# A decoder layer on one core: three fold pieces moved behind the gate's ranks, and quantizing's second step on ScalarE

## The chip, the cores and the metric

The kernel runs on one core of one Trainium2 chip, as one launch. The metric is the device time of an execution in microseconds; lower is better. It is given as the median of several runs.

## What is computed

Two layers of a decoder on four sequences of 512 rows with 256 features, in float32. Each of six blocks adds to the running `x` a function of its normalized rows:

```python
x = x + _L0_attn_ref(_layernorm(x, axis=-1), ...)     # causal mixing of 16 heads, a gated running sum
x = x + _L0_xattn_ref(_layernorm(x, axis=-1), ctx_768, ...)   # 16 heads, softmax over 512 keys
x = x + _L0_ffn_ref(_layernorm(x, axis=-1), ...)      # 8 experts and 4 "zero" experts, top two of a gate
x = x + _L1_attn_ref(_layernorm(x, axis=-1), ...)     # a gated recurrence over time
x = x + _L1_xattn_ref(_layernorm(x, axis=-1), ctx_768, ...)   # ternary weights, 8-bit activations
x = x + _L1_ffn_ref(_layernorm(x, axis=-1), ...)      # 8 linear experts, top two of a gate
```

Two pieces of it matter here. The experts of the last block have no function between their two matrices, so `(h @ w_in.T) @ w_out.T` can be computed with one 256 x 256 matrix per expert, the "folded" weight `w_in.T @ w_out.T`. And each linear map of the fifth block rounds its input to steps of the largest absolute value of the whole tensor:

```python
i_scale = jnp.maximum(jnp.max(jnp.abs(x)), 1e-08) / 127.0
qx = jnp.clip(jnp.round(x / i_scale), -128.0, 127.0)
out = jnp.einsum('...i,oi->...o', qx, qW) * (w_scale * i_scale)
```

The maximum is needed before the first value can be rounded, which makes each such map a stage of its own.

## The kernel before, in words

The program is written as Python functions that emit instructions. A scheduler then decides, for each engine, in which order its instructions stand in its queue; only instructions marked "in program order" (`pinned` matmuls, `move` transfers) keep the order of the source among themselves. Each engine runs its queue strictly in order. Tiles come from pools with a fixed number of buffers, and an instruction that needs a buffer waits until the last reader of its former content is done. So a small edit can move instructions elsewhere as well.

The stages, with their times in the profiled execution:

- **The frame** (`l0_mixers`, to about 560 us). The first two blocks are interleaved in 16 units `u` (sequence `u // 4`, a quarter of the heads each). A unit has eight slots `n`; in each slot scores are computed (PE, L588), reduced for their maximum (DVE `tops`, L927) and passed through an exponential (ACT `e`, L930); further work is hung into slots by `after(n, f, ...)` (around L1202). From unit 11 on this includes the **fold**: `fold_piece(i)` is one of four pieces of the folded weight of expert `i // 4`, four matmuls that the trace lists as eight rows (L588 `fold<-w_outT,w_in`). `fetch_fold(e)` loads the two weights of expert `e` (2 MB, four transfers in SP's queue, L595); they have two buffers, so expert `e` is fetched when expert `e - 2` has its last piece done. After an expert's fourth piece ACT copies the sum out (`folded`, L1091) and SP stores it (`far_folded`). Units 11 to 15 take four pieces each, 0 to 19, in slots 0, 1, 2 and 7.
- **The tail of the frame** (about 560 to 609 us, from L1352). The last sequence's results are added to `x`; then `Places` sorts its rows to the experts of the third block: `norm` (DVE), `transpose`, `score` (the gate's matmuls), `pick` (top two; `top_two`, L1399 to L1428, in which ACT computes `tt_share` at L1426 from DVE's `tt_gap`), `rank` (PE counts with `ranks`, L588; DVE then works out each row's place, L1550 to L1568), and `put` (GpSimd scatters rows into a table, one indirect transfer for 128 rows and one of its two experts). Between them stand pieces 20 to 22, 23, and, after the puts and `fetch_fold(7)`, pieces 24 to 31. A fence (L1597) waits for all the puts; the first expert's rows are read from the table behind it (L1632).
- **The experts** (`l0_experts`, 609 to 794 us). For each of eight experts: read its 640 rows, transpose them (PE `eturn` L1637, DVE copy `eht` L1638), first matrix (PE `ef<-eht,sw`), ACT `eact`, second matrix (PE `ef<-sw,eact`), DVE copy `ey` (L1668), store. Interleaved with it, through generators, stand the ternary weights (`Ternary`: a sum on DVE, a total on PE, comparisons on DVE) and the image side of the fifth block (`images`): quantize the context (`q_ctx`), matmuls `vis`, their maxima (`vis_tops`, L1897), quantize (`q_vis`), matmuls `img`, maxima and means, quantize (`q_img`), matmuls for the keys.
- **Gather and recurrence** (`l1_attn`, to about 948 us): rows are gathered from the table, then the fourth block.
- **The text side** (`l1_fuse`, to 1069 us): quantize the text (`q_txt`), matmuls `fused`, two attentions over the image keys (`bsc`, `bet`, `bav`), then quantize the result (`q_cat`).
- **The hidden stage** (`l1_hidden`, to about 1119 us): 32 matmul groups `hid`, for each a Relu on ACT (L2169) and a maximum on DVE (`hid_tops`, L1897); after the last of them quantize (`q_hid`, 16 slices of 128 x 1024, four a sequence), matmuls `bf`, and their sum into `x` (L2183).
- **The last block** (`l1_ffn`, to the end): the folded weights are read back (L2192), then norm, gate and the `y` matmuls.

`Steps.quantize(dst, src, tmp, on_act)` rounds in two steps through a temporary: multiply and add a large constant (which rounds), and subtract it again. The temporary `q_tmp` has two buffers in the stages where `on_act` is used. With `on_act` the first step runs on ACT, otherwise on DVE; the second runs on DVE in both cases. `on_act` is set for every other slice: two of the four slices of the text, two of `q_cat`, eight of the sixteen of `q_hid`. `q_ctx`, `q_vis`, `q_img` and the small `q_mean` don't use it.

Of the kernel before, what the change touches and what calls it, by code (L numbers as in the profile page):

```python
# [9 lines left out]
F32 = mybir.dt.float32  # L10
# [3 lines left out]
AF = mybir.ActivationFunctionType  # L14
# [4 lines left out]
P = 128  # L19
# [15 lines left out]
MAGIC = 12582912.0  # L35
# [6 lines left out]
class Kernel:  # L42


    def __init__(self, ctx, tc, a, out):
        self.ctx, self.tc, self.nc, self.a, self.out = ctx, tc, tc.nc, a, out
        nc = self.nc
        self.const = ctx.enter_context(tc.tile_pool(name="const", bufs=1))
        self.keep = ctx.enter_context(tc.tile_pool(name="keep", bufs=1))
        self.h_pool = ctx.enter_context(tc.tile_pool(name="h", bufs=2))  # L50
        self.small = ctx.enter_context(tc.tile_pool(name="small", bufs=4))
        self.open_psum()
        ctx.callback(self.close_psum)


        self.tops = self.keep.tile([P, 4 * NB, QT, 4], F32, name="tops")
        self.fine = self.keep.tile([P, 2 + 4 * (NB - 2)], F32, name="fine")

        self.most = self.keep.tile([P, 1], F32, name="most")

        self.rows = self.keep.tile([P, 2, NT], I32, name="rows")
        self.shares = self.keep.tile([P, 2, NT], F32, name="shares")
        self.fence = self.keep.tile([1, 1], F32, name="fence")
        self.puts = []
        self.table = ctx.enter_context(tc.tile_pool(name="table", bufs=1, space=bass.MemoryType.DRAM)).tile(
            [STAY + 2 * N, D], F32, name="table"
        )

        self.x = self.keep.tile([P, NT, D], F32, name="x_sb")
        self.load_x(0)  # L70

        self.ident = self.const.tile([P, P], F32, name="ident")
        make_identity(nc, self.ident)
        self.ones = self.const.tile([P, P], F32, name="ones_pp")
        nc.gpsimd.memset(self.ones, 1.0)
        self.magic = self.const.tile([P, 1], F32, name="magic")
        nc.gpsimd.memset(self.magic, MAGIC)


        self.by_head = self.head_of(self.const, "by_head", [P, 4, 16], [[P, 4], [-32, 16]], 1)  # L80
        self.iota12 = self.const.tile([P, 12], F32, name="iota12")
        nc.gpsimd.iota(
            self.iota12, pattern=[[1, 12]], base=0, channel_multiplier=0, allow_small_or_imprecise_dtypes=True
        )
        self.iota12_up = self.const.tile([P, 12], F32, name="iota12_up")
        nc.vector.tensor_scalar_add(self.iota12_up, self.iota12, 64.0)
# [454 lines left out]
def l0_mixers(k):  # L541
# [18 lines left out]
    nc, tc, a = k.nc, k.tc, k.a  # L560
    k.close_psum()
    far_folded(k)
    with ExitStack() as es:
# [11 lines left out]
        def bank(name):  # L575
            return ps_misc.tile([P, 512], F32, tag="bank", name=name)
# [7 lines left out]
        def pinned(out, pairs, start=True, stop=True):  # L584

            for i, (lhs_t, rhs) in enumerate(pairs):
                tc.keep_in_program_order(
                    nc.tensor.matmul(  # L588
                        out, lhs_t, rhs, start=start and i == 0, stop=stop and i == len(pairs) - 1
                    )  # L590
                )

        def move(dst, src):

            dma = nc.sync.dma_start(dst, src)  # L595
            tc.keep_in_program_order(dma)
            return dma
# [13 lines left out]
        ctxs, w, bias, padded = {}, {}, {}, {}  # L611
# [453 lines left out]
        def fetch_fold(e):  # L1065

            folds[e] = []
            for name in ("w_in", "w_outT"):
                t = k.fold_w.tile([P, 8, D], F32, tag=name, name=f"{name}_{e}", bufs=2)
                src = a[name][e].rearrange("(c p) d -> p c d", p=P)  # L1070
                for j in (0, 4):
                    move(t[:, j : j + 4], src[:, j : j + 4])
                folds[e].append(t)

        def fold_piece(i):

            e, c, j4 = i // 4, i // 2 % 2, i % 2 * 4
            if i % 4 == 0:
                folds[e].append(bank(f"fold_{e}").rearrange("p (c d) -> p c d", d=D))
                if e + 1 < 7:  # L1080
                    fetch_fold(e + 1)
            w_in, w_out, ps = folds[e]
            pinned(
                ps[:, c, :],
                [(w_in[:, j, c * P : (c + 1) * P], w_out[:, j, :]) for j in range(j4, j4 + 4)],
                j4 == 0,
                j4 == 4,
            )
            if i % 4 == 3:
                folded = k.fold_w.tile([P, DC * D], F32, tag="folded", name=f"folded_{e}", bufs=2)  # L1090
                nc.scalar.copy(folded.rearrange("p (c d) -> p c d", d=D), ps)  # L1091
                move(k.far_folded[e], folded)
# [122 lines left out]
        units = 4 * NB  # L1215
        for u in range(units + 1):
# [6 lines left out]
            def after(n, f, *args):  # L1223
                then[n].append((f, *args))
# [10 lines left out]
            if u == FOLDING:  # L1235

                mixers.close()
                k.fold_pool = ExitStack()
                k.fold_w = k.fold_pool.enter_context(tc.tile_pool(name="fold_w", bufs=2, side="right"))
                k.places = Places(  # L1240
                    k, k.fold_pool.enter_context(tc.tile_pool(name="places", bufs=1, side="right")),
                    move, bank, turn, pinned, new_ht,
                )
                after(7, fetch_fold, 0)
            elif u > FOLDING:
                if u < units:
                    for j, n in enumerate((0, 1, 2, 7)):
                        after(n, fold_piece, 4 * (u - FOLDING - 1) + j)
                g = k.places
                if u == 11:  # L1250
                    after(1, g.norm, 0)
                    for c in range(DC):
                        after(4 + c, g.transpose, 0, c)
                    after(5, g.norm, 1)
                    after(6, g.score, 0, (0, 1))
                elif u == 12:
                    for c in range(DC):
                        after(1 + c, g.transpose, 1, c)
                    after(3, g.score, 1, (0, 1))
                    after(4, g.pick, (0, 1))  # L1260
                    after(7, g.rank, (0, 1))
                elif u == 13:
                    for i in range(QT):
                        after(2 + i, project, 2, i)
                        after(3 + i, g.put, 0, i, weighing)
                    after(7, g.norm, 2)
                elif u == 14:
                    for c in range(DC):
                        after(1 + c, g.transpose, 2, c)
                    for i in range(QT):  # L1270
                        after(3 + i, g.put, 1, i, weighing)
                    after(3, g.score, 2, (2,))
                    after(3, g.pick, (2,))
                    after(6, g.rank, (2,))
                elif u == 15:
                    for i in range(QT):
                        after(3 + i, g.put, 2, i, weighing)
# [78 lines left out]
            xt = k.x[:, (NB - 1) * QT + i, :]  # L1356
            nc.vector.tensor_add(xt, xt, outs["xo"][:, i, :])
        places, last = k.places, NB - 1
        for i in range(20, 23):
            fold_piece(i)  # L1360
        places.norm(last)
        for c in range(DC):
            places.transpose(last, c)
        places.score(last, (last,))
        places.pick((last,))
        fold_piece(23)
        places.rank((last,))
        for i in range(QT):
            places.put(last, i)
        fetch_fold(7)  # L1370
        for i in range(24, 32):
            fold_piece(i)
# [6 lines left out]
FOLDING = 10  # L1379
# [473 lines left out]
class Steps:  # L1853
# [25 lines left out]
    def quantize(self, dst, src, tmp, on_act=False):  # L1879

        nc, p = self.k.nc, src.shape[0]
        t = tmp.tile(list(src.shape), F32, tag="q_tmp", name="q_tmp")
        if on_act:
            nc.scalar.activation(t, src, AF.Identity, scale=self.inverse[:p], bias=self.k.magic[:p])
        else:
            nc.vector.tensor_scalar(t, src, self.inverse[:p], MAGIC, ALU.mult, ALU.add)
        nc.vector.tensor_scalar_sub(dst, t, MAGIC)

    def scale_with(self, weight, pool, name):
        s = pool.tile([P, 1], F32, name=name)  # L1890
# [350 lines left out]


FAST = [l0_mixers, ahead, l0_experts, l1_attn, l1_xattn, l1_ffn]
GENERAL = [l0_attn, l0_xattn_clamped, ahead, l1_images, l0_ffn, l1_attn, l1_xattn, l1_ffn]

# [110 lines left out]
```

## Time and profile before

| what | value |
| --- | --- |
| runs: median (lowest to highest) | 1257.15 us (1253.43 to 1259.84) |
| the profiled execution: its time / its span | 1259.12 us / 1257.4 us |
| mean granted clock of TensorE | 0.887 of full speed |
| busy: PE / DVE / ACT / POOL | 79% / 65% / 33% / 15% |
| a fold piece (eight rows) | 1.99 us in the frame's end |
| quantize, first step, 128 x 1024: DVE / ACT | 748 ns / 1240 ns |
| quantize, second step on DVE | 688 ns |

The names of the engines: PE is TensorE's matmul (PEld its weight load), DVE is VectorE, ACT is ScalarE, POOL is GpSimd, SP is SyncE, whose queue issues most transfers. A row of the view by stretch gives, for a window in us from the span's start, its length and then the busy time of each engine with its count of instructions, the granted clock of TensorE, the busy share of the DMA engines and what they moved. A row of the timeline gives start, duration, engine, line, operation, output and inputs, the number of instructions in it, and in brackets how long the engine had been idle before and what ended that. A row of a tile's view gives the shortest, median and longest duration in ns and the starts of the first and last.

### The profile page before, as it was taken

The numbers are of one execution on the slowest core, as the hardware profiler recorded it, in microseconds if no ns is written. First come the engines' busy times: TensorE is split into PE (matmuls) and PEld (weight loads), VectorE is DVE, ScalarE is ACT, GpSimd is POOL, SyncE is SP. The second block draws the span as 40 slices with busy tenths as digits, with TensorE's granted clock in tenths as the row PEclk, the third lists the DMA queues.
The fourth block names the chain that finished last, engine by engine and source line by source line (L and its number), as shares of the span: only waits on it lengthen the run. The fifth ranks groups of instructions, "written<-read, shape, count | busy, mean of one in ns | idle before, by whom it ended". The sixth has DMA issues, their size and how long they took to land. (4 is left out here: it accounts for less than half of the span.)

```text
span 1257.4 us, 12049 instructions
## 1 busy us (share of the span) xinstructions
PE 996.7 (79%) x3865; PEld 560.1 (45%) x3871; DVE 815.4 (65%) x1980; ACT 417.0 (33%) x716; POOL 188.0 (15%) x224
## 2 busy tenths in 40 slices
PE   5889578688965999788689999336686777779997
PEld 1454333243332556547566677213453433254443
DVE  5776697777679767634365951437756665986564
ACT  4513345545443464430101421023323433820000
POOL 5431112113113002221000000450001220000000
PEclk9989787888976999888899999668887998879999
DMA  5385515333443635544557261220001110020000
GB/s 155 94 266 208 149 38 174 116 112 120 143 145 111 205 118 162 179 137 141 171 172 208 85 225 64 79 76 1 0 1 38 47 37 17 0 68 1 33 17 20
DMA packets 90779, 129.97 MB, mean 103 GB/s; under 512 B 20268, under 2 KB 61740, under 8 KB 90700
## 3 DMA queue, kind: packets, MB, share of 16 engines
q1 hardware_dynamic: 84544, 111.29, 28.3%
q0 software_dynamic: 6144, 17.83, 4.1%
q8 instruction: 33, 0.54, 0.2%
q14 instruction: 38, 0.31, 0.1%
q10 hardware_dynamic: 20, 0.00, 0.0%
HBM read 86.56 MB, written 42.53 MB: 103 GB/s over the span
## 5 line engine op out<-in xcount | busy, mean ns | idle before, releaser
L930 ACT ACTIVATE e<-score,tops 128x512 f32<-128x512 f32 x256 | 161.4, 685 | 171.8 <-DVE tops L927 99.3
L927 DVE TENSOR_REDUCE tops<-score 128x2 f32<-128x1024 f32 x128 | 155.8, 1219 | 44.4 <-PE score L588 39.6
L212 PE MATMUL y<-folded_sb,fht 128*128 128x512 f32 x256 | 113.4, 603 | 0.0
L588 PE MATMUL score<-query,key 64*128 64x512 f32 x256 | 67.8, 532 | 24.7 <-ACT e L930 21.3
L2212 DVE SCALAR_TENSOR_TENSOR x_sb<-y,tt_w,x_sb 128x256 f32<-128x256 f32 x128 | 61.9, 483 | 38.3 <-PE y L212 35.0
L965 PE MATMUL av<-e,weighed 128*32 128x512 f32 x512 | 77.8, 648 | 5.7 <-POOL weighed L953 5.7
L212 PE MATMUL ef<-sw,eact 128*128 128x256 f32 x320 | 79.4, 387 | 2.4 <-DVE ey L1668 2.4
L212 PE MATMUL ef<-eht,sw 128*128 128x320 f32 x256 | 76.7, 440 | 0.6 <-ACT eact L1657 0.6
L212 PEld LDWEIGHTS y<-folded_sb,fht 128*128 128x128 f32 x256 | 49.2, 194 | 60.3 <-issue 60.2
L588 PEld LDWEIGHTS score<-query,key 64*128 64x128 f32 x256 | 25.2, 197 | 100.9 <-ACT e L930 51.9
L212 PEld LDWEIGHTS ef<-sw,eact 128*128 128x128 f32 x320 | 58.7, 193 | 12.9 <-DVE ey L1668 5.1
L588 PE MATMUL fold<-w_outT,w_in 128*128 128x256 f32 x256 | 63.3, 397 | 0.5 <-PE fold L588 0.5
L203 PE MATMUL turn<-ident,h 128*128 128x128 f32 x64 | 13.7, 364 | 62.5 <-DVE h L190 42.1
L588 PE MATMUL o<-o_wT_sb,qk 128*128 128x256 f32 x128 | 47.1, 531 | 20.3 <-DVE qk L826 20.3
L212 PEld LDWEIGHTS ef<-eht,sw 128*128 128x128 f32 x256 | 47.8, 192 | 17.4 <-ACT eact L1657 1.2
L1657 ACT ACTIVATE eact<-ef 128x640 f32<-128x640 f32 x32 | 22.3, 702 | 100.0 <-PE ef L212 100.0
L588 PEld LDWEIGHTS fold<-w_outT,w_in 128*128 128x128 f32 x256 | 48.3, 196 | 9.5 <-issue 2.6
L588 PEld LDWEIGHTS o<-o_wT_sb,qk 128*128 128x128 f32 x128 | 32.8, 268 | 33.9 <-DVE qk L826 23.6
L212 PE MATMUL f<-aht,W_fT_sb 128*128 128x512 f32 x96 | 47.5, 644 | 0.1
L1638 DVE COPY eht<-eturn 128x256 f32<-128x256 f32 x40 | 16.8, 421 | 42.4 <-PE eturn L1637 42.2
L1740 POOL DMA_INDIRECT got<-table,rows x32 | 30.4, 949 | 85.9 <-DVE neg_b L1732 76.5
L179 DVE BATCH_NORM_STATS2 ln_st<-x_sb 128x6 f32<-128x256 f32 x96 | 38.1, 412 | 5.8 <-DMA x_sb<-in_x 3.8
(394 smaller groups left out, 1812.0 us busy)
## 6 DMA issues: line engine op xcount, KB each, us to landing
table<-zeros POOLq DMA_DIRECT2D x8, 1152.0 KB
factors<-far SPq DMA_DIRECT2D x64, 128.0 KB
key<-far_k SPq DMA_DIRECT2D x16, 512.0 KB
query<-far_q SPq DMA_DIRECT2D x16, 512.0 KB
w_in<-in_w_in SPq DMA_DIRECT2D x16, 512.0 KB
w_outT<-in_w_outT SPq DMA_DIRECT2D x16, 512.0 KB
rows<-table SPq DMA_DIRECT2D x8, 640.0 KB
table<-ey SPq DMA_DIRECT2D x8, 640.0 KB
```

Of the source, the lines that this page charges most:

```text
L179: nc.vector.bn_stats(st[:, i, :], s)
L203: nc.tensor.transpose(ps[:, i * P : (i + 1) * P], h[:, i, c * P : (c + 1) * P], self.ident)
L212: self.nc.tensor.matmul(out, lhs_t, rhs, start=(i == 0), stop=(i == len(pairs) - 1))
L588: nc.tensor.matmul(out, lhs_t, rhs, start=start and i == 0, stop=stop and i == len(pairs) - 1)
L927: nc.vector.tensor_reduce(top, ps, AX.X, ALU.max, negate=True)
L930: nc.scalar.activation(e[:, i, :], ps[:, i, :], AF.Exp, bias=top[:, i : i + 1])
L965: nc.tensor.matmul(avs[u][32 * h : 32 * h + 32, :], weighed[u % 2][:, j, h, :], es_of[u, h // 2, j][:, h % 2, :], start=(j == 0), stop=(j ...
L1638: nc.vector.tensor_copy(ht[:, :, i * P : (i + 1) * P], ps)
L1657: nc.scalar.activation(act[:, f, :].rearrange("p (j t) -> p j t", j=2), ps[:, :, :half], AF.Silu)
L1740: nc.gpsimd.indirect_dma_start(out=got[t, which], out_offset=None, in_=k.table, in_offset=bass.IndirectOffsetOnAxis(ap=k.rows[:, which, t ...
L2212: nc.vector.scalar_tensor_tensor(xt, ps[:, e, :], w[:, i, e4 + e : e4 + e + 1], xt, ALU.mult, ALU.add)
```

## The change

Three edits. A constant tile `less` holds the negative of the rounding constant. In the frame, unit 14 takes pieces 12 to 14 and unit 15 pieces 15 and 16, so 17 pieces instead of 20 lie in the units; in the tail pieces 17 to 19 stand where 20 to 22 stood, 20 where 23 stood, and 21 to 23 behind the ranks and puts, ahead of the fetch for expert 7. And where `on_act` is set, quantizing's second step is an Identity activation on ACT with `less` as its bias, instead of DVE's subtraction. From line 77 on every line of the changed kernel stands two to seven lines lower.

```diff
         self.magic = self.const.tile([P, 1], F32, name="magic")
         nc.gpsimd.memset(self.magic, MAGIC)
+        self.less = self.const.tile([P, 1], F32, name="less")
+        nc.gpsimd.memset(self.less, -MAGIC)
...
             elif u > FOLDING:
                 if u < units:
-                    for j, n in enumerate((0, 1, 2, 7)):
-                        after(n, fold_piece, 4 * (u - FOLDING - 1) + j)
+
+                    first = 4 * (u - FOLDING - 1) - (u == units - 1)
+                    for j, n in enumerate((0, 1, 2, 7)[: min(4, units + 1 - u)]):
+                        after(n, fold_piece, first + j)
...
         places, last = k.places, NB - 1
-        for i in range(20, 23):
+        for i in range(17, 20):
             fold_piece(i)
         places.norm(last)
         for c in range(DC):
             places.transpose(last, c)
         places.score(last, (last,))
         places.pick((last,))
-        fold_piece(23)
+        fold_piece(20)
         places.rank((last,))
         for i in range(QT):
             places.put(last, i)
+        for i in range(21, 24):
+            fold_piece(i)
         fetch_fold(7)
         for i in range(24, 32):
             fold_piece(i)
...
         if on_act:
             nc.scalar.activation(t, src, AF.Identity, scale=self.inverse[:p], bias=self.k.magic[:p])
+            nc.scalar.activation(dst, t, AF.Identity, bias=self.k.less[:p])
         else:
             nc.vector.tensor_scalar(t, src, self.inverse[:p], MAGIC, ALU.mult, ALU.add)
-        nc.vector.tensor_scalar_sub(dst, t, MAGIC)
+            nc.vector.tensor_scalar_sub(dst, t, MAGIC)
```

## The prediction

> **What bounds the kernel now.** I read the page's busy shares first (PE 79%, DVE 65%, ACT 33%), then busy time by stretch, because the share is an average over stages with different limits.
>
> ```profile
> core 0: us, PE busy (x) PEld busy (x) DVE busy (x) ACT busy (x) POOL busy (x), PEclk, DMA share, GB/s
> 528.00:547.00 19.00, 17.52 (x101) 10.27 (x99) 12.27 (x26) 9.50 (x17) 6.89 (x8) 1.00 0.50 163
> 547.00:560.00 13.00, 9.88 (x54) 4.92 (x55) 3.06 (x13) 3.37 (x7) 2.16 (x3) 0.74 0.65 208
> 586.00:609.00 23.00, 14.80 (x69) 12.54 (x70) 3.96 (x28) 1.17 (x2) 8.38 (x10) 0.92 0.81 266
> 690.00:735.00 45.00, 41.05 (x204) 28.54 (x207) 40.75 (x77) 16.52 (x23) 1.05 (x3) 1.00 0.34 115
> ...
> 1069.00:1091.00 22.00, 16.87 (x57) 5.32 (x56) 21.48 (x33) 21.18 (x32) 0.00 (x0) 0.97 0.00 0
> 1091.00:1120.00 29.00, 19.39 (x128) 13.60 (x128) 26.74 (x73) 9.93 (x8) 0.35 (x1) 0.78 0.01 1
> ```
>
> PE has idle time in the frame's end and in the tail (rows two and three). In 690–735 PE and DVE are both nearly full, so order decides. In 1069–1091 DVE and ACT are full together; in 1091–1120 DVE is, with ACT two thirds idle. Then the tail, PE first, then ACT, then DVE:
>
> ```profile
> 581.07 3.76 PE L588 MATMUL fold<-w_outT,w_in 128*128 128x256 f32 x8
> 586.38 0.39 PE L588 MATMUL ranks<-both,before 128*128 128x48 f32 x2 [1.55 <-DVE both L1533]
> ...
> 594.46 7.14 PE L588 MATMUL fold<-w_outT,w_in 128*128 128x256 f32 x32 [0.50 <-PE fold L588]
> 608.94 0.66 PE L1637 MATMUL eturn<-ident,rows 128*128 128x128 f32 x2 [7.33 <-DMA rows<-table]
> ```
> ```profile
> 584.91 0.58 ACT L1091 COPY folded<-fold 128x512 f32<-128x512 f32 x1 [6.91 <-issue]
> 585.39 0.21 ACT L1426 ACTIVATE tt_share<-tt_gap 128x4 f32<-128x4 f32 x1
> ```
> ```profile
> 583.53 0.15 DVE L1415 TENSOR_TENSOR tt_gap<-top,top 128x4 f32<-128x4 f32 x1
> 585.63 0.24 DVE L1428 TENSOR_SCALAR shares<-tt_share 128x4 f32<-128x4 f32 x2 [1.54 <-ACT tt_share L1426]
> ```
>
> tt_gap is done at 583.68, but tt_share is queued behind the copy of the fold, which waits for piece 23; DVE loses 1.54 us and the ranks with it. From the ranks hang the rows, the puts, the fence, and the read of the first expert's rows, for which PE stands idle 7.33 us.
>
> **The frame.** A piece is 8 matmul rows: 1.99 us, 2.53 at the slow clock. Three leave (525.71, 535.29, 544.83): 6.5 us of PE. PE doesn't set the end there: around these pieces it waits for POOL's `weighed` (1.09), DVE's `low` (0.87) and `diag` (2.30), so removal is worth no 6.5 us. In the new order DVE's `low` stands behind a row reduce, which can delay an `av` group by about 1.6; on the other side the 2.30 wait may shrink. Bounds −1.6 to +2. A rule speaks against the move: 548–552 is mostly idle and 552–556 ran at clock 0.50, where 32 `av` took 5.50 us (eight took 1.06 at full clock, so 32 should take 4.2). The Trainium skill, "TensorE: Matmul & The Clock Gate", Part 1, says that an idle window of some 3.4 us puts the array at half clock and that a busy one of that length restores it: filler taken out makes one more such window likely. By the row nothing is added, since that loss is already there; by the rule one more half-clock window costs an estimated 1.7. I take +0.5, nearer the row.
>
> **The tail.** Pieces 17–19 replace 20–22 in 569.4–574.8, beside DVE's normalization; piece 20 replaces 23. With tt_share ahead of the copy in ACT's queue, the ranks come 1.5 earlier (584.9). Pieces 21–23 (3 × 1.79 = 5.4) then run to 590.7, 24–27 to 597.8. SP: the fetch of expert 7's weights needs piece 23 and moves from 585.96 to some 591; 2 MB at the 350 GB/s of this stretch is 6 us, about 1 to land, so 28–31 start near 598.3 and end at 605.5. Rows land at 608.9 − 1.5 = 607.4: the 5.4 us are covered by PE's 7.33 of idle (without it they would cost all 5.4). SP's later loads (w1, w2 of expert 0, the copies of folded weights) stay ahead of the rows' read; the puts on POOL keep their eight 1.27 us slots but share the DMA engines with the fetch (±1). One thing takes the gain back: on PE the new order puts W_d2vT's total ahead of the first eturn. That weight is issued 0.41 us behind the rows, then DVE reduces it (0.67) and a matmul follows: eturn at about 607.4 + 0.4 + 0.7 + 0.5 = 609.0 against 608.94. Net 0, from −1.5 (no wait) to +2 (late rows).
>
> **The experts, whose source is untouched.** The compiled queues of the two kernels differ here: the image chain (q_ctx, vis, q_vis, img, q_img, keys) is interleaved about one expert earlier.
>
> ```profile
> L212 PE MATMUL vis<-q_ctx,W_d2vT_q x16: 376/377/381, 693.1 to 702.6; 96*128 96x512 bf16 x16
> ```
> ```profile
> L212 PE MATMUL img<-q_vis,W_imgT_q x15: 376/379/389, 707.6 to 717.2; 128*128 128x512 bf16 x15
> L1887 DVE TENSOR_SCALAR q_vis<-q_tmp x4: 683/695/695, 706.9 to 711.6; 128x1024 bf16<-128x1024 f32 x4
> ```
>
> Before, the first vis (693.13) to the first key (725.3) takes 32.2 us; PE has 31.2 us of work queued between, DVE about as much: balanced, 1 us lost. I add up the same durations along the new queues. PE has 23.7 us between first vis and first key, as less expert work lies between. DVE, from the first q_ctx to the first q_img: three pairs q_tmp/q_ctx 4.3, eight vis tops 5.4, two ey and two eht copies 1.9, step and its POOL reduce 1.2, first q_vis pair 1.4; then three pairs 4.3, eight img tops 5.4, four img_mean 5.0, copies 1.9, step 1.5, q_img 1.4: 33.7 in all. It leads by about 3.7, as q_ctx is ready while PE still has 5.8 us of other matmuls ahead of vis (less a 0.7 copy and the 1.4 pair). PE is starved 33.7 − 23.7 − 3.7 = 6.3 instead of 1.0: +5.3, and with 0.2 for a shorter cover elsewhere I take +5.5. The starved PE can't run expert 4 ahead: its eturn copies on DVE stand behind six img tops and three img_mean. The PE-only work behind the keys grows (77.6 us for 61.8), with DVE idle, so nothing is won back. Bounds: −3, if PE's waits ahead of vis (9.6 us before, 3.32 of them one eturn on DVE) shrink and nothing starves; +13, if the lead isn't there and those waits grow by 4.
>
> **Quantizing.** Twelve second steps leave DVE (0.69 each, 8.3 us) for ACT. ACT's f32-to-bf16 form isn't in the trace; nearest is the first step on ACT:
>
> ```profile
> L1887 DVE TENSOR_SCALAR q_hid<-q_tmp x16: 677/688/696, 1092.8 to 1113.3; 128x1024 bf16<-128x1024 f32 x16
> ...
> L1884 ACT ACTIVATE q_tmp<-hid,magic,hid_inverse x8: 1239/1240/1242, 1092.1 to 1110.0; 128x1024 f32<-128x1024 f32 x8
> ```
>
> Text: ACT's chain is 4 × 1.24 = 5.0 from 950.3, ready at 955.3, PE needs the last at 955.8: 0. Cat: ACT runs 4 × 1.24 from 1064.3, to 1069.3; the first Relu of `hid`, queued behind, began at 1068.68, and the stage after it is full on ACT and DVE: +0.6. Hid: before, 16 slices took from 1092.05 to 1114.0; now DVE has 1.44 per pair of slices and ACT 2.48, ACT sets the pace: 8 × 2.48 = 19.8, to 1112, with a little slack 1112.5. The last x_sb (1117.35) follows the last slice by 3.3, and the fetch of the folded weights (1118.69) hangs on it: −1.2. The Trainium skill, "ScalarE: Activation LUTs", on what ACTIVATE costs, has 280 ns + 0.833 per element with a pointer bias, and back-to-back overlap of 93 ns: an estimated 1.13 for the new step instead of the row's 1.24. By the page cat is 0 and hid −2.5, quantizing −2.5 in all; by the row −0.6. I take the row: the second step reads what the first has just written, so the page's overlap can't be counted on here; bounds −2.5 to +1. The y stage, PE-full, is untouched.
>
> **Sum.** 0.5 + 0 + 5.5 + 0.6 − 1.2 = +5.4 on the profiled execution's 1259.12 (span 1257.4 and 1.7 around it), so 1264.5. That execution lies 1.97 above the median of the runs, 1257.15: predicted 1262.5.
>
> **Rivals.** (a) *Clearly slower.* The same starvation in full: DVE gives no lead, because its ctx reduces stand between the eht copies there (as PE's 3.32 wait before vis does now). PE then loses 10 rather than 6.3 and 1–4 more ahead of vis: experts +11, sum +11, 1268. It decides from a lead under 2.5 us. For: the interleave of tops and eht in the new order; against: DVE was busy only 29 of 50 us just before. (b) *Faster.* PE's waits in the expert stage shrink because the early chain fills them, and the tail keeps its 1.5: experts −3, tail −1.5, frame −1, quantizing −2: −7.5, 1249.7. It decides from experts at 0 or below. For: 9.6 us of waits ahead of vis, ACT's copy that does leave the path; against: the sum of 33.7 on DVE. (c) *No effect*: experts 0 to +2, the other terms cancel; 1257. For: only little of the order in other stages moves.
>
> **Chances.** Forecast (its own range 1259 to 1266) 0.36, (a) 0.27, (b) 0.20, (c) 0.17. A measurement of this kernel tells about 0.5% (6.3 us) from no change: slower means over 1263.4, faster under 1250.9. The forecast straddles the upper bound, half of it on either side. Slower: (a) and that half, 0.45. Faster: nearly all of (b), 0.18. Same: the rest, 0.37. The range takes in most of (b) and of (a): 1250 to 1273.
>
> **What would show it.** Frame: first `att` work of the tail within 2 us of before. Tail: ranks before 585.5, PE's wait for rows about 2 us instead of 7.33, eturn within 2 us of 609. Experts: first vis near 689, first key near 719, PE's gaps between them waiting for q_vis, img and q_img. Hid: ACT back to back at about 1.24, last x_sb 1 us earlier relative to the stage's start. Wrong if the experts' stretch (609 to 794) doesn't get longer, if ACT's second step is far from 1.24, or if the rows land late.

## The result and the profile after

The changed kernel took 1269.42 us (median of 6 runs, 1266.45 to 1271.05) against 1256.54 us for the kernel before: a ratio of 1.0106, 95% interval 1.0078 to 1.0134. So it is slower by 1.1%, 13 us. The profiled execution took 1269.73 us with a span of 1268.0, 10.6 over the span of before. It lies outside the forecast's own range (1259 to 1266), at rival (a), 1268, and inside the stated range of 1250 to 1273.

Where the 10.6 us went, by the starts of the same instructions in both traces (the stretch from the first Relu to the first quantize of `hid`, not listed, took 23.3 in both):

| stretch | before | after | difference | predicted |
| --- | --- | --- | --- | --- |
| start to unit 13's `low` | 498.5 | 495.8 | -2.7 | 0 |
| unit 13's `low` to the first `xo` (frame's end) | 61.2 | 66.0 | +4.8 | +0.5 |
| first `xo` to the ranks | 26.7 | 23.6 | -3.1 | -1.5 |
| ranks to the first `eturn` | 22.5 | 25.5 | +3.0 | +1.5 |
| first `eturn` to the first gather (experts) | 190.0 | 203.7 | +13.7 | +5.5 |
| first gather to the first `fused` | 152.9 | 151.8 | -1.1 | 0 |
| first `fused` to the first Relu of `hid` | 116.9 | 117.3 | +0.4 | +0.6 |
| first quantize of `hid` to the first `y` | 34.2 | 30.8 | -3.4 | -1.2 |
| first to last `y` | 122.1 | 121.2 | -0.9 | 0 |

The first row is not the change's: the first units hold the same instructions, and the first `low` starts anywhere from 159.5 to 162.6 us in the twelve other traces, with the old fold and the new.

**The experts.** The rows by stretch of before and then of after, from the first eturn to the first gather:

```profile
608.90:798.90 190.00, 171.24 (x779) 127.04 (x782) 99.21 (x182) 40.93 (x57) 1.05 (x3) 0.97 0.45 144
```
```profile
610.80:814.50 203.70, 177.81 (x782) 129.97 (x782) 99.80 (x181) 41.25 (x57) 1.08 (x4) 0.94 0.41 131
```

PE runs nearly the same number of instructions, but it is busy 6.6 us longer with them, at a clock of 0.94 instead of 0.97, and it idles 25.9 us instead of 18.8, 7.1 more. These two are the 13.7. The timelines of the changed kernel show where, PE first, then DVE:

```profile
657.42 0.69 PE L1643 MATMUL eturn<-ident,rows 128*128 128x128 f32 x2 [4.29 <-DVE eht L1644]
...
680.78 0.44 PE L1643 MATMUL eturn<-ident,rows 128*128 128x128 f32 x2 [3.12 <-DVE eht L1644]
...
718.17 0.93 PE L214 MATMUL ef<-eht,sw 128*128 128x320 f32 x2 [3.75 <-DVE eht L1644]
719.09 1.22 PE L214 MATMUL ef<-sw,eact 128*128 128x256 f32 x2
...
722.36 4.82 PE L214 MATMUL ef<-sw,eact 128*128 128x256 f32 x14
```
```profile
652.55 4.48 DVE L1854 SCALAR_TENSOR_TENSOR W_f1T_q<-W_f1T_sb,W_f1T_half,W_f1T_low 128x4096 bf16<-128x4096 f32 x1
656.95 0.42 DVE L1644 COPY eht<-eturn 128x256 f32<-128x256 f32 x1
...
679.12 1.28 DVE L1904 TENSOR_REDUCE ctx_tops<-ctx_all 96x1 f32<-96x512 f32 x2 [3.37 <-DMA ctx_all<-in_ctxT]
680.31 0.41 DVE L1644 COPY eht<-eturn 128x256 f32<-128x256 f32 x1
...
714.25 3.46 DVE L1986 TENSOR_REDUCE img_mean<-img_t 128x2 f32<-128x1024 f32 x3
717.63 0.15 DVE L1869 TENSOR_REDUCE img_one<-img_tops 128x1 f32<-128x8 f32 x1
717.70 0.41 DVE L1644 COPY eht<-eturn 128x256 f32<-128x256 f32 x1
```

In each of the three places PE waits for a small eht copy, 0.41 us, which stands on DVE behind something else: a comparison of 4.48 us, the context's maxima, which had themselves waited 3.37 us for their transfer, and the image's sums. The second has its like before (3.32 us ahead of vis, also behind the context's maxima); the first and the third are new. After the third wait two `ef<-sw,eact` rows take 1.22 us, where two take 0.59 to 0.60 in the same trace at full clock, and fourteen take 4.82, where fourteen took 3.27 at 634.58. The rows by stretch behind the three waits show half the clock:

```profile
653.87:660.70 6.83, 3.28 (x10) 2.45 (x11) 4.94 (x5) 0.00 (x0) 0.00 (x0) 0.50 0.35 108
681.18:684.59 3.41, 3.41 (x10) 2.35 (x9) 2.25 (x6) 0.00 (x0) 0.00 (x0) 0.50 1.05 359
718.72:725.55 6.83, 6.46 (x21) 4.20 (x21) 6.62 (x13) 0.78 (x1) 0.00 (x0) 0.50 0.14 56
```

Together they are 17.1 us at half clock. Before, the clock was at half for 6.7 us from the first eturn (6.8 in the changed kernel), for 3.4 from 653.12, behind a wait of 2.93, and for the last 2.4, and nowhere else in the stage: the wait of 3.32 was followed by full clock. So the clock's loss came on top of the waits here, but not every wait of this length brings it.

**The frame's end**, PE in the changed kernel:

```profile
531.96 0.37 PE L939 MATMUL low<-ident,low 128*4 128x128 f32 x1 [2.57 <-DVE works L1569]
532.13 3.71 PE L590 MATMUL fold<-w_outT,w_in 128*128 128x256 f32 x8
...
541.72 1.94 PE L967 MATMUL av<-e,weighed 128*32 128x512 f32 x8 [2.87 <-POOL weighed L955]
```

Unit 14's `low` on PE waits 2.57 us, as DVE reduces it only at 531.64, behind two row maxima of unit 15 and the ranks' work (`works`, which the row names, is the reduce right behind it); before, DVE did it at 527.08, right behind unit 14's last maximum. A piece then takes 3.71 instead of 1.99, a group of `av` 1.94 instead of 1.06.

**The tail**, ACT and PE:

```profile
584.41 0.21 ACT L1432 ACTIVATE tt_share<-tt_gap 128x4 f32<-128x4 f32 x1 [4.34 <-DVE tt_gap L1421]
```
```profile
585.39 0.49 PE L590 MATMUL ranks<-both,before 128*128 128x48 f32 x2 [0.39 <-DVE both L1539]
...
600.57 7.41 PE L590 MATMUL fold<-w_outT,w_in 128*128 128x256 f32 x32 [2.31 <-issue]
610.63 0.38 PE L214 MATMUL W_d2vT_total<-W_d2vT_sum,ones_pp 96*128 96x1 f32 x2 [2.66 <-DVE W_d2vT_sum L1842]
```

tt_share follows tt_gap at once; PE's wait ahead of the ranks is 0.39 instead of 1.55. PE waits 2.31 ahead of pieces 28 to 31, most likely for expert 7's weights (fetched from 592.49 on; the row itself names no cause), and 2.66 for the first ternary weight's sum instead of 7.33 for the rows.

**Quantizing of `hid`**, by the view of its output:

```profile
L1894 DVE TENSOR_SCALAR q_hid<-q_tmp x8: 679/690/696, 1107.7 to 1124.4; 128x1024 bf16<-128x1024 f32 x8
L1891 ACT ACTIVATE q_hid<-q_tmp,less x8: 1147/1148/1150, 1108.2 to 1125.1; 128x1024 bf16<-128x1024 f32 x8
```

Half of the second steps are now ACT's, 1.148 us each. ACT runs from 1106.94 to 1126.27 without a break: 19.3 us for 16 slices that took 22.0. The `y` stage, 0.9 shorter, goes with it: 121.1 to 121.5 us in all eleven traces with this step on ACT, 122.1 in the two without (before and experiment 1). Why isn't shown.

### The profile page after: what moved, and what is told of

Same layout as the page of the kernel before. It is cut to its first block, busy times and chain, and to the rows that moved or that the text cites. A ratio compares the mean times of both kernels' runs of the same rounds, so it can differ in the third digit from the quotient of the medians.

```text
span 1268.0 us, 12062 instructions
## 1 busy us (share of the span) xinstructions
PE 1002.4 (79%) x3871; PEld 561.7 (44%) x3871; DVE 811.0 (64%) x1968; ACT 431.2 (34%) x728; POOL 187.9 (15%) x225
## 5 line engine op out<-in xcount | busy, mean ns | idle before, releaser
L590 PE MATMUL o<-o_wT_sb,qk 128*128 128x256 f32 x128 | 45.2, 515 | 19.3 <-DVE qk L828 19.3
L955 POOL TENSOR_TENSOR weighed<-v,weighed 128x256 f32<-128x256 f32 x16 | 10.4, 647 | 209.8 <-ACT weighed L954 189.9
```

Of the source, the lines that this page charges most:

```text
L590: nc.tensor.matmul(out, lhs_t, rhs, start=start and i == 0, stop=stop and i == len(pairs) - 1)
```

## The experiments

Each was timed in five rounds against the kernel before on the same chip. The first four share a chip, so do the next four, and the last three. On the chip of the second four the kernel before took 1225 us, on the others 1257 to 1259, so times are compared within a set, by ratios, and a difference in us is the ratio's; where ratios of two sets stand side by side, that comparison is weaker.

**1. The move alone** (quantizing as before).

```diff
-            nc.scalar.activation(dst, t, AF.Identity, bias=self.k.less[:p])
+            nc.vector.tensor_scalar_sub(dst, t, MAGIC)
```

> The fold pieces moved, quantizing as before. The changed kernel was 12.9 us over the kernel before; its stages in the two traces: frame +2.1 (first xo of the last sequence), tail -0.2 (first eturn), experts +13.7 (first eturn to first gather), cat +0.4, hid quantize -3.4, last stage -0.9. Theory A (the new order of the image chain against the experts, which comes with the move alone, costs the time; quantizing gains): about +16.5 on the kernel before, 1.013, with the stretch from the first eturn to the first gather near 204 us. Rival B (the move is nearly free, the second step on ACT costs the time): within 2 us of the kernel before.

Measured 1.0151 (1.0126 to 1.0175), +19 us, with the experts' stretch at 203.7 us as in the changed kernel, and the first `xo` 67.2 us behind unit 13's `low`. Rival B falls: the move costs all of it.

**2. Quantizing alone** (fold as before).

```diff
+            nc.scalar.activation(dst, t, AF.Identity, bias=self.k.less[:p])
         else:
             nc.vector.tensor_scalar(t, src, self.inverse[:p], MAGIC, ALU.mult, ALU.add)
-        nc.vector.tensor_scalar_sub(dst, t, MAGIC)
+            nc.vector.tensor_scalar_sub(dst, t, MAGIC)
```

> Quantizing's second step on ACT alone, fold as before. Theory A: 3 to 4 us faster than the kernel before (0.997), all of it in the hidden stage's quantize (16 slices in 18.5 us instead of 22), experts' stretch 190 as before. Rival B: slower by 10 us or more. Rival C (the hid gain is lost again in the last stage, whose start waits for the folded weights): within 1 us of the kernel before.

Measured 0.9959 (0.9942 to 0.9976), 5 us faster; from the first quantize of `hid` to the first `y` 31.1 us instead of 34.2. Rivals B and C fall.

**3. The three pieces ahead of the gate.**

```diff
-        for i in range(17, 20):
+        for i in range(17, 23):
             fold_piece(i)
...
-        fold_piece(20)
+        fold_piece(23)
         places.rank((last,))
...
-        for i in range(21, 24):
-            fold_piece(i)
```

> As the changed kernel, but the three pieces stand ahead of the gate (17 to 22 before the normalization, 23 before the ranks) instead of behind the ranks. The compiled order of the experts' stage is then that of the kernel before. Theory A (order): the experts' stretch falls back from 203.7 to about 190 us, while the three extra pieces ahead of the gate, which nothing covers, cost about 5 us in the tail: first eturn near 616, the whole about +2 to +4 us on the kernel before. Rival D (the experts are slowed by something carried over from the frame, such as the clock or later transfers, not by their order): the stretch stays at 203, the whole about +17.

Measured 1.0030 (1.0015 to 1.0045), +3.8 us; the experts' stretch is 188.8 us. The pieces left the same slots of the frame, and only the tail and the compiled order behind it differ: rival D falls. From the first `xo` to the ranks it took 28.9 us instead of 23.6. (Its profiled execution was the fastest of its 22 runs, 8 us under their median, so only its stretches are used. Its tail cost less than the 5 us expected: from the first `xo` to the first eturn it took 51.0 us, against 49.1 in the changed kernel.)

**4. The image chain emitted later.**

```diff
+            images_of, others = others, iter(())
             for e in range(8):
+                if e == 2:
+                    others = images_of
                 expert(e)
```

> As the changed kernel, but the image chain is emitted from the third expert on instead of the first, so that between first img and first key PE has 48 expert matmul groups queued where the changed kernel has 15 and the kernel before 25. Theory A (PE is starved by a chain that is short of cover): the stretch of the experts falls by 7 to 12 us, to 192 to 197, the whole to about 1260; the waits for eht of W_f1T's comparison (4.3 us) and of the context's maxima (3.1) stay. Rival E (the waits ahead of the chain and the clock make the loss, not the chain): it falls by less than 3 us.

Measured 1.0017 (1.0003 to 1.0032), 11 us less than the changed kernel's ratio; the stretch is 190.6 us. First img to first key is 28.7 us, as more expert work now lies there, and first key to gather 55.4 instead of 93.8. Rival E falls, and theory A's 192 to 197 was too careful.

**5. One edge of order**: the first ternary weight's sum on DVE behind the first eht copy.

```diff
-        nc.vector.tensor_reduce(total, w, AX.XY, ALU.add, apply_absolute_value=True)
+        summed = nc.vector.tensor_reduce(total, w, AX.XY, ALU.add, apply_absolute_value=True)
+        if name == "W_d2vT" and hasattr(k, "first_turn"):
+            k.tc.add_manual_dep(
+                summed.ins,
+                k.first_turn.ins.name,
+                mybir.DependencyInfo(mybir.DependencyClass.NoSync, mybir.DependencyReason.DATA),
+                reason="behind the first rows",
+            )
```

> The changed kernel with one edge of order more: the sum of the first ternary weight on DVE goes behind the first eht copy, so its total no longer stands ahead of the first eturn on PE. The compiled order of the weights and of the image chain against the experts is then again that of the kernel before. Theory A (order alone): the first eturn comes about 2 us earlier after the ranks (23.5 us instead of 25.5), the stretch from it to the first gather falls from 203.7 to about 190, and the whole to about 4 us under the kernel before (0.997), that is 16 under the changed kernel. Rival D (the moved pieces themselves load the experts' stage): at most the 2 us of the first eturn.

Measured 1.0032 (1.0020 to 1.0044). The one edge gives the compiled queues the old interleave of weights and image chain: in the traces DVE's 182 instructions of the stage stand in the very order of the kernel before, in experiments 3, 9 and 10 too. The stretch is 187.6 us: the experts' step is settled as one of order. But the whole missed the 0.997. The ranks-to-eturn part didn't shorten (27.3 us): the rows had landed at 603.75, but PE was still at pieces 28 to 31, behind the later fetch and in part at half clock (8.83 us; 7.41 in the changed kernel), and the eturn then waited for ACT's copy of that sum:

```profile
596.99 8.83 PE L590 MATMUL fold<-w_outT,w_in 128*128 128x256 f32 x32 [2.88 <-issue]
606.54 0.44 PE L1643 MATMUL eturn<-ident,rows 128*128 128x128 f32 x2 [0.72 <-ACT folded L1093]
```

And the frame showed its own cost. From unit 13's `low` to the first `xo` it took 60.0 us, against 53.1 in both kernels of this set with the old frame (6 and 8): 6.9.

**6. ACT's second step for `hid` only** (kernel before otherwise).

```diff
-                steps.quantize(q_hid[:, cut, :], hid[:, cut, k.cols(b)], wk, on_act=f2 % 4)
+                steps.quantize(q_hid[:, cut, :], hid[:, cut, k.cols(b)], wk, on_act=f2 % 4, both=True)
```

> The kernel before with the second step on ACT in the hidden stage's eight slices only; text and concatenated slices as before. If the cat step's place ahead of the first Relu costs 0.6 to 0.9 us, this is that much faster than the version with all twelve on ACT (0.9959): 0.995 to 0.9955, the first Relu of hid 116.9 us behind the first fused matmul instead of 117.8. If the twelve belong together, 0.996 to 0.997.

Measured 0.9967 (0.9956 to 0.9977). The first Relu comes 117.0 us behind the first fused matmul, 0.8 earlier than in experiment 2, as expected; in the whole the two can't be told apart.

**7. Without the image's sums**: the image's mean is left at zero, so the kernel computes something else.

```diff
-    for b in range(NB):
-        nc.vector.tensor_reduce(k.img_mean[:, :, b], img[:, :, k.cols(b)], AX.X, ALU.add)
+    nc.vector.memset(k.img_mean, 0.0)
```

> The changed kernel without the four sums over img on DVE (the image mean is left at zero, so the result differs), 4.7 us of DVE work out of the chain between img and the keys. Its weights and image chain keep the early order. Theory A (DVE is what PE waits for there): first img to first key falls from 17.5 to about 13 us and the whole by 3 to 5 us, to 1.006. Rival (PE waits for something else): under 1 us.

Measured 1.0059 (1.0039 to 1.0079), 0.0047 under the changed kernel's ratio, though on another chip. First img to first key is 13.7 us instead of 17.5, and the stretch of the experts 191.1: taking 4.7 us of DVE work out gave 12.6 back there. Not all of it is the sums' doing: other instructions moved on DVE as well, and besides the half clock behind the third wait that at the stage's start (6.8 us) and the one behind the second wait are missing too. The 3.8 between img and key are DVE's.

**8. Quantizing alone, image chain later**: the edits of 2 and 4.

> The kernel before with all twelve second steps on ACT and the image chain emitted from the third expert on. Its chain has 48 expert groups of cover between img and keys instead of 25. In the kernel before some 7 us of waits lie behind the first key and 1 between vis and key; if they come from the chain, 2 to 4 us are gained on the 0.9959 of quantizing alone, 0.993 to 0.994; if not, 0.996.

Measured 0.9946 (0.9924 to 0.9967). The stretch is 187.8 us. The 0.0013 that it is under experiment 2 is inside the intervals.

**9. Unit 14's `low` early**, on top of experiment 5: its reduce is emitted behind the unit's last row maximum (`lower`), the rest of `least` where it was.

```diff
                 for f, *args in then[n]:
                     f(*args)
+                if u == units - 2 and n == 7:
+                    lower(u)
```

> As the version with the first ternary sum behind the first eht copy (1.0032), and with unit 14's low put on DVE directly behind that unit's last row reduce, as in the kernel before; in the changed kernel it stands behind two row reduces of unit 15 and the work on the ranks. The three pieces stay out of the frame. In the traces the stretch from unit 13's low to the first xo is 61 us with all pieces in the frame and 66 without them on one chip, 53 and 60 on another. Theory F1 (the new place of low delays PE, and with it the weights and av of unit 14): 4 to 5 us come back, ratio 0.999 to 1.000. Theory F2 (PE loses its filler and runs at the half clock behind the idle time): under 1.5 us come back, 1.002 to 1.0035.

Measured 0.9966 (0.9949 to 0.9983). The pieces are still out of the frame. Its PE timeline and its row from the first eturn to the gather:

```profile
532.43 0.27 PE L947 MATMUL low<-ident,low 128*4 128x128 f32 x1
532.54 1.89 PE L590 MATMUL fold<-w_outT,w_in 128*128 128x256 f32 x8
...
539.57 1.06 PE L975 MATMUL av<-e,weighed 128*32 128x512 f32 x8 [3.07 <-POOL weighed L963]
```
```profile
608.90:798.30 189.40, 171.34 (x779) 127.57 (x782) 99.03 (x182) 40.94 (x57) 1.05 (x3) 0.97 0.45 144
```

`low` waits for nothing, the piece behind it takes 1.89 instead of 3.71, and `low` to `xo` is 61.8 us. From ranks to eturn it took 24.3 us, where experiment 5 took 27.3, as PE ran the pieces of the tail at full clock again. F1 is right in kind and too small (it expected 0.999 to 1.000; the 3 us of the tail were not in it), F2 falls as the cause: without any filler the time is back. PE still waits 3.07 for `weighed`; the first `av` group behind it runs at full clock, only the next at half (1.94 at 541.29).

**10. Dummy pieces in the three empty slots**, on top of experiment 5.

```diff
+        def filler():
+
+            w_in, w_out, _ = folds[3]
+            ps = bank("filler")
+            pinned(ps[:, :D], [(w_in[:, j, :P], w_out[:, j, :]) for j in range(4)])
```

> As the version with the first ternary sum behind the first eht copy (1.0032), with a dummy piece (four matmuls on weights that are there, result unread) in each of the three slots that the moved pieces left. PE then has more work in all than in the kernel before, by three pieces. Theory F (the frame's end needs these matmuls, by order or as cover for the clock): the frame falls back by 5 to 8 us and the whole, though it does more, to 0.997 to 0.9995; what is left over the 0.9959 of quantizing alone is the tail, 2 to 4 us. Rival (the frame's end is only limited by DVE and ACT, fillers only add): 1.003 to 1.006.

Measured 0.9977 (0.9958 to 0.9997): three pieces more work on PE, and faster than without them. `low` to `xo` is 62.6 us; the tail's 27.2, as in experiment 5, stayed. But with the dummies the compiled order also puts `low` early again, so this run alone can't tell cover from order; experiment 9 does.

**11. The fastest**: the edits of 6 and 4 on the kernel before.

> A version meant to be the fastest: fold as in the kernel before, second step on ACT in the hidden stage only, image chain emitted from the third expert on. Sum of the gains that the runs showed for each: hidden stage 0.9967, later images 1.5 to 2.5 us: 0.994 to 0.9955.

Measured 0.9935 (0.9911 to 0.9958), 1250.13 us against 1258.79: 8.7 us faster than the kernel before, and faster than the changed one.

## Why the prediction was right or wrong

**The sign and the place were right.** The largest term was said to be the experts' stage, whose source is untouched, and experiments 3, 4 and 5 show it there and as order. The size was half or less: +5.4 forecast, +10.6 in the traces, +12.9 in the medians. Errors of opposite sign offset each other in part, which is luck: experts and frame were put 12.5 us too low, quantizing 2.4 too high.

**Experts, +5.5 predicted, +13.7 measured.** The step "PE is starved 33.7 - 23.7 - 3.7 = 6.3 instead of 1.0" held: from first vis to first key PE idled 5.5 us (30.9 less 25.4 busy) against 1.5 before. All the added idle time of the stage is 7.1, because PE waited more ahead of vis too (11.8 against 9.9; 4.29 of it for an eht copy behind W_f1T's comparison) and behind the key (8.6 against 7.4). What failed is the term that isn't in the sum: the same matmuls took 6.6 us longer. The prediction cited the clock rule of the Trainium skill ("TensorE: Matmul & The Clock Gate", Part 1) for the frame and left it out here, where it forecast the longer waits itself. In this trace waits of 3.1 to 4.3 us were followed by 3.4 to 6.8 us at half speed; the clock nearly doubled the price of the waits, 6.6 on 7.1. The stage's time at half clock grew from 12.5 to 24.1 us, and half of the growth, an estimated 5.8, is most of the 6.6.

**Frame, +0.5 predicted, +4.8 measured** (6.9 on another chip). The step "by the row nothing is added ... I take +0.5, nearer the row" failed. The new place of `low` on DVE was seen and priced at 1.6; it cost 2.57 of waiting and then half clock from 530.99 to 537.82 and, behind the wait for `weighed`, from 541.23 to 548.06. So the rule was nearer than the row, though not in its figure: the page has an idle window of some 3.4 us, and here the clock fell 1.6 us into a wait of 2.57. But the pieces taken out are not what slowed PE: experiment 9 has no filler and no loss. There `low` waits for nothing and the clock stays full until 540.5: the order set the wait, and the half clock came with the wait.

**Tail, 0 predicted, -0.1 measured.** Both halves came, and nearly cancelled; that the sum is so near 0 is in part luck. From `lg` to `both` DVE took 3.1 us instead of 4.8, the predicted 1.5 of tt_share. The rest of the -3.1 is largely the profiled execution of before: with the old tail experiments 2 and 6 took 24.6 and 23.6 from `xo` to the ranks, so against them the gain is 0 to 1. Behind the ranks, 2.66 of waiting for the first weight's total was the predicted term. Experiment 9 removed that wait and still took 24.3 from ranks to eturn, 22.1 to 23.7 with the old tail: there PE waits 1.24 for the rows, which land later, perhaps as puts and rows share the DMA engines with the later fetch; that was given as ±1 and wasn't tried alone. And "the 5.4 us are covered" held only narrowly: pieces 28 to 31 ended at 608.0, not 605.5, and in experiments 5 and 10 they and the copy of their sum, not the rows, kept PE from the eturn.

**Quantizing, -0.6 predicted, about -3 measured** in the traces, -5 in the runs of experiment 2. ACT's second step took 1.148 us: the row said 1.24, the estimate from the Trainium skill ("ScalarE: Activation LUTs", "What ACT_TABLE_LOAD costs", its paragraph on ACTIVATE) 1.13. Here the page was nearer, and choosing the row was the error; its overlap of 93 ns didn't come where it was doubted: a second step started 1.26 to 1.28 us after the first step that it reads, which takes 1.24. So ACT's chain was 19.3 us, 0.5 less than the 19.8 of the sum, and the sum had added 0.5 of slack that wasn't there (and booked −1.2 where its own 1114.0 and 1112.5 give −1.5). Behind the last slice another 0.8 came, from its end to the first `y` (11.4 us instead of 12.2). Cat was right: +0.4 in the traces, 0.8 between experiments 2 and 6.

**The sum.** With order repaired in both places (experiment 9), the changed kernel runs at 0.9966, where quantizing alone runs at 0.9959 on another chip, the same within their intervals. The moved pieces as such cost nothing that can be told, which leaves room for some 4 us; the bulk of the 19 us that experiment 1 shows (1.0126 to 1.0175) comes from what they do to the order of other work.

## What to carry to other kernels

Where a scheduler orders the queues, compare the queues of both kernels over the whole program, since work moved in one stage can reorder another: here a weight's sum that stood one place earlier on DVE moved a whole chain forward by one expert. Then look for short copies that PE needs behind long work on DVE. And where a new wait of PE of some 3 us is forecast, give it a second term for matmuls at half clock behind it, as a range from nothing to as much again: 7.1 us of added idle time came with 6.6 of slower matmuls here, while the 3.32 us ahead of vis before cost no clock.

## What the runs showed of the hardware that was not expected

Chips differ by stage, not evenly: on the chip of experiments 5 to 8 the stretch from the first gather to the first `fused` took 130 to 132 us, on the others 151 to 153, with the same instructions, and unit 14 with the old fold 25.3 us instead of 28.5 to 30.0; the stretches of the hidden stage and of the last block agreed within 1 us. Most of the 20 us can be pointed at. In the first normalizations behind the gather DVE runs a chain of small instructions, here in the changed kernel and then in experiment 5:

```profile
852.78 0.16 DVE L165 TENSOR_TENSOR ln_u<-ln_u,ln_half 128x4 f32<-128x4 f32 x1 [1.24 <-DVE ln_u L164]
854.18 0.16 DVE L166 SCALAR_TENSOR_TENSOR ln_y<-ln_u,ln_y 128x4 f32<-128x4 f32 x1 [1.24 <-DVE ln_u L165]
```
```profile
817.96 0.16 DVE L165 TENSOR_TENSOR ln_u<-ln_u,ln_half 128x4 f32<-128x4 f32 x1
818.15 0.16 DVE L166 SCALAR_TENSOR_TENSOR ln_y<-ln_u,ln_y 128x4 f32<-128x4 f32 x1
```

From 843 to 858 us they start 1.40 us apart, on the other chip 0.20, with the same 0.16 us of work each; in all nine traces outside that set 11 to 14 starts of the stretch are spaced so, in the set of experiments 5 to 8 at most 2. From the `ln_mv` at 835.25 to the `h` that the chain leads to it takes 23.8 us, in experiment 5 4.6. The waits end on nothing that the profile shows but the instruction ahead, long done. Why isn't shown.
